# Attention over four batches: values times probabilities in four column tiles, row sums on GpSimd

## The chip, the cores and the metric

The kernel runs on one core of a Trainium2 chip, in f32 throughout. The metric is the time of one execution on the device in microseconds; the time before is the median of 3 runs, 4841.11 us (4838.23 to 4847.09).

The engines are called TensorE (PE in the profile, PEld for its weight loads), VectorE (DVE), ScalarE (ACT), GpSimd (POOL) and SyncE (SP, which here only issues DMAs). Each engine works its own queue in order.

## The reference

The reference is a chain of four residual layers on an input of 4 batches x 384 channels x 64 x 64. Only layer 0 and the part of layer 1 that runs beside it matter here. Layer 0, cut to what matters:

```python
xn  = layer norm over the 96 channels of x[:, :96]
qkv = einsum('oc,bchw->bohw', w_qkv, xn), scaled and shifted
q, k, v = 16, 16 and 96 channels, N = 4096 positions
attn = softmax(einsum('bcn,bcm->bnm', q, k) * scale, axis=-1)
out  = einsum('bcn,bmn->bcm', v, attn)
y    = w_proj @ relu(concat([out, x[:, 96:]])), scaled and shifted
x    = x + y
```

Layer 1 is a matrix product, a filter on 8 x 8 blocks in the Fourier domain, a depthwise 3 x 3 convolution with a gated GELU, and a second matrix product.

## The kernel before

`phase_a` runs layers 0 and 1. For each batch `b`, `side_by_side` interleaves two generators: `attention(b)`, which yields 64 times, and `others(b)`, which holds layer 1 of batch `b - 1` (`layer1`), the statistics of the next batch (`x_norm`) and its queries, keys and values (`qkv`). The order in which each engine gets its instructions is then set by a scheduler at build time, from dependences, priorities and its own estimates of cost. So batch 0 of attention runs beside little else, batches 1 to 3 run beside layer 1 of the batch before, and layer 1 of batch 3 runs alone at the end of the phase.

A step of `attention` is a pair (i, c): a block i of 512 query positions and a group c of 4 x 128 key positions. `scores` (L805) makes 4 matmuls of 32 rows each that run at once (L811), into one PSUM tile of four banks, and ScalarE takes the exponential of the halves into `probs`, a tile of 2048 columns in two buffers (L819). Scores are one step ahead of the products. The maximum is not subtracted inside the loop, so the softmax needs only a sum of the exponentials over the keys and one division per block.

Products and sums exist in two forms:

- Batches 1 to 3: four matmuls a step of 128 x 128 x 512 (L929). The stationary operand `vt` has 128 columns: 96 of values and 32 of ones (`wv` has ones in its last row and columns), so rows 96 to 127 of the result `av` hold the sum of the probabilities. At the end of a block `finish` (L897) takes the reciprocal of those rows (L901) and multiplies three quarters of `av` by it (L904). `av` alternates between the two PSUM buffers of tag "a".
- Batch 0: `products` (L827) computes the 96 value columns alone, as three pieces of 32 columns for each of the four groups of 128 keys, 12 matmuls a step. The four column tiles of TensorE work on four of them at once, in three rounds that `PLAN` sets out, into two PSUM tiles `av_0` and `av_1` (L834). The sum over the keys is made apart: `add_up` (L842) adds the two halves of `probs` into `acc_p` on VectorE (L848, L850, L851), and at the end of a block the two halves of that (L854). `evacuate` (L856) copies the pieces out of PSUM on ScalarE and VectorE (L860 to L863), `invert` (L866) sums `acc_p` over the partitions with ones (L870) and takes the reciprocal (L878), and `finish_tiles` (L881) spreads it by matmuls (L886), adds the pieces (L893) and multiplies (L894).

Both end in `layer0_end` (L949): ReLU of the other channels on ScalarE, three groups of three matmuls (L965), the addition to the residual on VectorE (L972), and a DMA issued by GpSimd (L975). These matmuls, those of layer 1 and those of `qkv` share one PSUM tag "m" with two buffers.

In `layer1`, `tile_norm` (L1043, VectorE), `tile_hidden` (L1051), `tile_filter` (L1066, L1068) and `tile_back` (L1076) fill a ring of three `bands`. `halo` copies rows between bands on GpSimd (L1089, L1090). `band_taps` applies nine taps for each of three channel blocks: the first on ScalarE (L1126), the others on VectorE (L1128: an instruction with two tensor inputs, band and acc). `band_out` multiplies, adds (L1148, L1149, L1152) and stores with a DMA issued by GpSimd (L1155).

At the end of the kernel, `boxes` adds rows with GpSimd (L2021, L2023) and VectorE (L2024 to L2034) side by side, and `conv7` builds band matrices on both (L1959).

Of the kernel before, what the change touches and what calls it, by code (L numbers as in the profile page):

```python
# [21 lines left out]
F32 = mybir.dt.float32  # L22
AF = mybir.ActivationFunctionType
ALU = mybir.AluOpType
# [4 lines left out]
NJ = 3  # L29
P = 128  # L30
PD = 96
# [250 lines left out]
class _Builder:  # L282
# [161 lines left out]
    def qkv_weights(self, pool):  # L444

        nc = self.nc
        w = self.wk("wq_raw", "lx", 2)[:, 0:PD]
        nc.scalar.dma_start(w, self.ins["w_qkv"])  # L450
        inv, shift = self.bn_scale_shift(
            "bn1", self.vec("bn1_m"), self.vec("bn1_v"), self.vec("bn1_g"), self.vec("bn1_b")
        )
        nc.vector.tensor_scalar(w, w, inv, None, ALU.mult)
        pt = self.pm("wq_pt")
        nc.tensor.transpose(pt[0:PD, 0:P], w, self.ident)
        wt = self.wk("wq_t", "ln", 3)[0 : PD + 1, 0:P]
        raw = self.wk("wq_rawt", "lx", 2)[0:PD, 0:P]
        nc.vector.tensor_copy(raw, pt[0:PD, 0:P])
        nc.vector.tensor_scalar(wt[0:PD, :], raw, self.vec("ln_w", PD), None, ALU.mult)  # L460
        pb = self.pm("wq_pb")
        nc.tensor.matmul(pb[0:1, 0:P], lhsT=self.vec("ln_b", PD), rhs=raw, start=True, stop=False)
        nc.tensor.matmul(pb[0:1, 0:P], lhsT=shift, rhs=self.ident, start=False, stop=True)
        nc.scalar.copy(wt[PD : PD + 1, :], pb[0:1, 0:P])

        self.wq4 = pool.tile([PD + 1, 4, 32], F32, tag="wq4", name="wq4")
        self.wk4 = pool.tile([PD + 1, 4, 32], F32, tag="wk4", name="wk4")
        self.wv = pool.tile([PD + 1, P], F32, tag="wv", name="wv")
        for t in (self.wq4, self.wk4, self.wv):
            nc.gpsimd.memset(t, 0.0)  # L470
        nc.gpsimd.memset(self.wk4[PD : PD + 1, :, 0:1], 1.0)
        nc.gpsimd.memset(self.wv[PD : PD + 1, PD:], 1.0)
        self.ones = pool.tile([P, 32], F32, tag="ones", name="ones")
        nc.gpsimd.memset(self.ones, 1.0)
        for g in range(4):
            nc.vector.tensor_copy(self.wq4[:, g, 1:17], wt[:, 0:16])
            nc.vector.tensor_copy(self.wk4[:, g, 1:17], wt[:, 16:32])
        nc.vector.tensor_copy(self.wv[:, 0:PD], wt[:, 32:P])
        self.wqk = pool.tile([PD + 1, 4, 32], F32, tag="wqk", name="wqk")
        nc.vector.tensor_copy(self.wqk[:, 0:3], self.wq4[:, 0:3])  # L480
        nc.vector.tensor_copy(self.wqk[:, 3], self.wk4[:, 3])
        self.score_bound(pool, wt)
# [220 lines left out]
    def qkv_tiles(self):  # L703


        q = [None] * 8
        k4 = self.big.tile([P, 8, P], F32, tag="k4", name="k4", bufs=2)
        vt = self.big.tile([P, 32, P], F32, tag="vt", name="vt", bufs=2)
        return q, k4, vt

    def qkv(self, b, q, k4, vt, tiles=(None,) * 8):
        nc = self.nc

        xc, xn = [None] * 8, [None] * 8
        xc[0] = self.centered(b, 0, tiles[0])
        yield 1.0
        xn[0] = self.layer_norm(xc[0])
        xc[1] = self.centered(b, 1, tiles[1])
        yield 2.0
        for i in range(8):  # L720
            if i + 2 < 8:
                xc[i + 2] = self.centered(b, i + 2, tiles[i + 2])
                yield 1.0
            if i + 1 < 8:
                xn[i + 1] = self.layer_norm(xc[i + 1])
                yield 1.0
            xa = xn[i]
            q[i] = self.big.tile([P, 512], F32, tag="q", name="q", bufs=9)
            m = self.pm("qk_m")
            nc.tensor.matmul(m, lhsT=self.wqk.rearrange("p g d -> p (g d)"), rhs=xa, start=True, stop=True)  # L730
            nc.scalar.copy(q[i][0:96], m[0:96])
            nc.scalar.copy(q[i][96:128], m[64:96])
            nc.sync.dma_start(
                q[i].rearrange("(g d) n -> g d n", g=4)[:, 0], self.shifts[b][:, i * 512 : (i + 1) * 512]
            )
            for g in range(4):
                nc.vector.tensor_copy(k4[32 * g : 32 * g + 32, i], m[96:128, g * P : (g + 1) * P])
            m = self.pm("v_m")
            mv = m.rearrange("p (c d) -> p c d", d=P)
            for c in range(4):  # L740
                nc.tensor.matmul(mv[:, c, :], lhsT=xa[:, c * P : (c + 1) * P], rhs=self.wv, start=True, stop=True)
            nc.vector.tensor_copy(vt[:, 4 * i : 4 * i + 4, :], mv)
            yield 2.8
# [14 lines left out]
    def maxima(self, b):  # L758
        nc = self.nc
        for _ in self.x_norm(b):  # L760
            pass
        q = self.big.tile([P, 32, P], F32, tag="vt", name="mx_q", bufs=2).rearrange("p (i a) n -> p i (a n)", i=8)
        q = [q[:, i] for i in range(8)]
        k = [self.probs.tile([P, 2048], F32, tag="p", name="mx_k") for _ in range(2)]
        for i in range(8):
            xa = self.layer_norm(self.centered(b, i))
            m = self.pm("mx_q_m")
            nc.tensor.matmul(m, lhsT=self.wq4.rearrange("p g d -> p (g d)"), rhs=xa, start=True, stop=True)
            nc.scalar.copy(q[i], m)
            m = self.pm("mx_k_m")  # L770
            nc.tensor.matmul(m, lhsT=self.wk4.rearrange("p g d -> p (g d)"), rhs=xa, start=True, stop=True)
            nc.vector.tensor_copy(k[i // 4][:, i % 4 * 512 : (i % 4 + 1) * 512], m)
        for i in range(8):
            mx = self.sm([P, 4, 2], "mx")
            for t in range(4):
                for u in range(2):
                    s = self.p4("mx_s")
                    for v in range(4):
# [4 lines left out]
                            start=True,  # L783
# [15 lines left out]
    def attention(self, b, q, k4, vt):  # L799
# [42 lines left out]
        def add_up(c, p):  # L842

            lo, hi = p[:, 0:1024], p[:, 1024:2048]
            if c == 0:
                t = self.blk.tile([P, NJ, 512], F32, tag="x", name="acc_p", bufs=1)
                self.acc = t[:, 0:2].rearrange("p a n -> p (a n)")
                nc.vector.tensor_add(self.acc, lo, hi)  # L848
            else:
                nc.vector.tensor_add(self.acc, self.acc, lo)  # L850
                nc.vector.tensor_add(self.acc, self.acc, hi)  # L851
            if c == 7:
                self.prob_sum = self.wk("sum_p", "acc", 5)
                nc.vector.tensor_add(self.prob_sum, self.acc[:, 0:512], self.acc[:, 512:1024])  # L854

        def evacuate(av):  # L856

            a, t = self.wk("av_a", "acc", 5), self.wk("av_t", "acc", 5)
            with tc.high_priority():
                nc.scalar.copy(t[0:32], av[0][96:128])  # L860
                nc.vector.tensor_copy(a[0:PD], av[0][0:PD])
                nc.scalar.copy(t[32:64], av[1][0:32])
                nc.vector.tensor_copy(t[64:96], av[1][32:64])  # L863
            return a, t
# [13 lines left out]
            nc.vector.reciprocal(rd, m[:, 0:P])  # L878
            return rd

        def finish_tiles(a, t, rd):  # L881

            xm = self.work.tile([P, NJ, 512], F32, tag="xm", name="xm", bufs=1)
            m = self.pm("rd_m")
# [9 lines left out]
            nc.vector.scalar_tensor_tensor(xm[0:PD, 0], t[0:PD], 0.0, m[0:PD], ALU.max, ALU.mult)  # L894
            return xm

        def finish(av):  # L897

            xm = self.work.tile([P, NJ, 512], F32, tag="xm", name="xm", bufs=1)
            rd = self.wk("av_rd", "rd", 1)  # L900
            nc.vector.reciprocal(rd[PD:P], av[PD:P])  # L901
            for g in range(3):
                at = slice(32 * g, 32 * g + 32)
                nc.vector.scalar_tensor_tensor(xm[at, 0], av[at], 0.0, rd[PD:P], ALU.max, ALU.mult)  # L904
            return xm

        st = self.stats_tile("xa_st")
        steps = [(i, c) for i in range(8) for c in range(8)]
        ahead = scores(*steps[0])
        done, end = None, iter(())  # L910
        close = finish if b else finish_tiles
        for n_step, (i, c) in enumerate(steps):
            p = ahead
            if n_step + 1 < len(steps):
                ahead = scores(*steps[n_step + 1])
            if b == 0:
                if c == 0:
                    av = self.pa("av_0"), self.pa("av_1")
                products(av, c, p)
                add_up(c, p)  # L920
                if c == 0 and done is not None:
                    done = *done, invert(self.prob_sum)
                if c == 7:
                    evacuated = evacuate(av)
            else:
                if c == 0:
                    av = (self.pa("av"),)
                for v in range(4):
                    nc.tensor.matmul(  # L929
                        av[0],  # L930
                        lhsT=vt[:, 4 * c + v, :],
                        rhs=p[:, v * 512 : (v + 1) * 512],
                        start=c == 0 and v == 0,
                        stop=c == 7 and v == 3,
                    )
                evacuated = av
            next(end, None)
            if c == 1 and done is not None:
                end = self.layer0_end(b, i - 1, close(*done), st)
            if c == 7:  # L940
                done = evacuated
            yield
        if b == 0:
            done = *done, invert(self.prob_sum)
        for _ in self.layer0_end(b, 7, close(*done), st):
            pass
        self.norm1 = self.norm_of_stats(st)

# [1153 lines left out]
```

## Time and profile before

| What | Value |
|---|---|
| Median of 3 runs | 4841.11 us |
| The profiled execution, its time | 4841.52 us |
| The profiled execution, its span | 4839.6 us |
| Attention, batch 0 | 40 to 458 us |
| Attention, batches 1, 2, 3 | 458 to 1017, to 1577, to 2139 us |
| Layer 1 of batch 3 alone | about 2139 to 2430 us |
| Granted TensorE clock, mean over the span | 0.95 |

In a table of stretches each row gives the start and end in us, the length, and for each engine its busy time with the number of instructions, then the granted TensorE clock, the busy share of the DMA engines and GB/s. In a group line stand the line of the kernel, the engine, the operation, the tile written and the tiles read, the shapes and the count, then the busy time in us, the mean ns of one, the idle time of the engine just before them, and what ended it. A line of a single source line gives the durations in ns as minimum/median/maximum and the first and last start. Every f32 matmul stands twice in the counts of TensorE.

### The profile page before, as it was taken

The page shows a single profiled execution, that of the slowest core. Times are in us where ns is not written, and L with a number is a line of the kernel's source. Part 1 is how long each engine was busy: PE and PEld are TensorE (multiplying, and loading weights), DVE is VectorE, ACT ScalarE, POOL GpSimd, SP SyncE. Part 2 cuts the span into 40 slices and gives each one's busy share as a digit, 9 for nine tenths or more (in the row PEclk, how much of TensorE's full clock was granted, in tenths as well). Part 3 has the DMA queues.
Part 4 walks back from the last instruction along what each step waited for, and adds up shares of the span by engine and source line. Part 5 has one row for each costly group of instructions (what it writes and reads, how often), then busy time and mean ns, then how long its engine had stood idle before and what let it go on. Part 6 is the DMA issues. An engine that isn't in the chain of part 4 may idle for free.

```text
span 4839.6 us, 49747 instructions
## 1 busy us (share of the span) xinstructions
PE 4399.5 (91%) x18445; PEld 2453.7 (51%) x18445; DVE 2892.0 (60%) x4647; ACT 1996.9 (41%) x2976; POOL 757.7 (16%) x643
## 2 busy tenths in 40 slices
PE   6999999999999999989987898699999997778888
PEld 2233444344443444435477787344444443678888
DVE  7766556645656455556867777555521113767898
ACT  4444444444444444336345566211133334763321
POOL 1000000000000000000044554000000001235544
PEclk9999999999999999989988999899999998788999
DMA  4312212111211111113168898776664444995776
GB/s 145 102 42 66 72 53 75 64 56 42 70 61 63 40 59 59 53 63 120 65 197 282 278 308 299 273 259 251 238 236 153 156 156 152 325 346 183 231 256 232
DMA packets 289663, 747.65 MB, mean 154 GB/s; under 512 B 22555, under 2 KB 123014, under 8 KB 277382
## 3 DMA queue, kind: packets, MB, share of 16 engines
q1 hardware_dynamic: 226744, 454.62, 29.4%
q0 software_dynamic: 36480, 167.01, 9.2%
q10 hardware_dynamic: 26190, 122.76, 6.4%
q8 instruction: 149, 2.44, 0.2%
q14 instruction: 100, 0.82, 0.1%
HBM read 442.04 MB, written 302.25 MB: 154 GB/s over the span
## 4 chain that ended last, share of the span: by engine, by line
PE 32%; DVE 7%; DMA 6%; ACT 3%; issue 2%; POOL 1%; SPq 0%; ACTq 0%; DVEq 0%; POOLq 0%
PE h_m L1658 10%; PE h_s L1604 10%; PE conv_m L1370 6%; PE conv_m L1972 2%; DMA c_d<-d 2%; DMA wmix<-in_mix_t 1%; DMA g_h<-h 1%; DVE toep L1959 1%; PE box_m L2050 1%; DVE in_x L2052 1%; DMA ax<-x 1%; DVE in_x L2062 1%; DMA unit_x<-x 1%; DVE box L2034 0%; ACT g_h L1908 0%
## 5 line engine op out<-in xcount | busy, mean ns | idle before, releaser
L819 ACT ACTIVATE probs<-sc_s 128x1024 f32<-128x1024 f32 x512 | 496.5, 1019 | 695.0 <-PE av L929 594.8
L929 PE MATMUL av<-probs,vt 128*128 128x512 f32 x1536 | 717.7, 604 | 0.0
L1128 DVE SCALAR_TENSOR_TENSOR acc<-band,vecs,acc 128x512 f32<-128x512 f32 x708 | 496.0, 745 | 44.9 <-POOL band L1089 39.6
L1658 PE MATMUL h_m<-f_h,cm_w_t 128*128 128x512 f32 x1152 | 497.3, 595 | 7.4 <-ACT f_h L1646 7.4
L1370 PE MATMUL conv_m<-toep,z 128*128 128x192 f32 (+1 forms) x2304 | 444.2, 354 | 9.5 <-DVE z L1299 9.4
L929 PEld LDWEIGHTS av<-probs,vt 128*128 128x128 f32 x1536 | 277.6, 192 | 339.6 <-issue 335.9
L1972 PE MATMUL conv_m<-toep,z 128*128 128x128 f32 x3072 | 395.5, 287 | 36.5 <-POOL toep L1959 15.8
L1370 PEld LDWEIGHTS conv_m<-toep,z 128*128 128x128 f32 x2304 | 408.5, 197 | 31.6 <-DVE z L1299 10.1
L1972 PEld LDWEIGHTS conv_m<-toep,z 128*128 128x128 f32 x3072 | 381.1, 203 | 38.4 <-POOL toep L1959 16.2
L1604 PE MATMUL h_s<-e_tok,cm_w_t 128*128 128x512 f32 x768 | 362.9, 595 | 4.2 <-DVE e_tok L1589 4.2
L1658 PEld LDWEIGHTS h_m<-f_h,cm_w_t 128*128 128x128 f32 x1152 | 220.4, 191 | 284.4 <-issue 273.3
L1666 DVE BATCH_NORM_STATS2 h_st<-f_h 128x6 f32<-128x512 f32 x96 | 66.5, 694 | 429.8 <-ACT f_h L1665 429.8
L811 PE MATMUL sc_s<-q,k 32*128 32x512 f32 x2048 | 307.1, 643 | 15.1 <-ACT probs L819 14.9
L1351 POOL TENSOR_TENSOR toep<-w,band 128x1280 f32<-128x1280 f32 x94 | 272.6, 2900 | 237.5 <-PE conv_m L1370 234.3
L1051 PE MATMUL t_m<-w_in_t,xb 128*128 128x384 f32 x768 | 282.0, 503 | 3.4 <-DVE coef L1068 3.2
L965 PE MATMUL proj_m<-xm,w_proj_t 128*128 128x512 f32 x576 | 270.3, 609 | 6.4 <-DVE xm L904 4.9
L1611 ACT COPY e_h<-h_s 128x1024 f32<-128x1024 f32 x96 | 97.2, 1012 | 400.2 <-PE h_s L1604 400.2
L1613 DVE BATCH_NORM_STATS2 h_st<-e_h 128x6 f32<-128x512 f32 x192 | 123.4, 685 | 204.9 <-ACT e_h L1611 204.7
L1604 PEld LDWEIGHTS h_s<-e_tok,cm_w_t 128*128 128x128 f32 x768 | 146.9, 191 | 187.9 <-issue 183.1
L1051 PEld LDWEIGHTS t_m<-w_in_t,xb 128*128 128x128 f32 x768 | 144.4, 194 | 141.6 <-issue 62.5
L972 DVE SCALAR_TENSOR_TENSOR x_res<-proj_m,bn_c,x_res 128x512 f32<-128x512 f32 x96 | 71.7, 747 | 240.2 <-PE proj_m L965 240.2
L1604 PE MATMUL h_s<-z,cm_w_t 128*128 128x512 f32 x384 | 196.7, 594 | 0.0
(423 smaller groups left out, 6396.3 us busy)
## 6 DMA issues: line engine op xcount, KB each, us to landing
d<-d_o ACTq DMA_DIRECT2D x48, 1024.0 KB
c_d<-d SPq DMA_DIRECT2D x48, 1024.0 KB
hid<-e_h ACTq DMA_DIRECT2D x16, 3072.0 KB
f_h<-hid SPq DMA_DIRECT2D x16, 3072.0 KB
x_in<-in_x SPq DMA_DIRECT2D x96, 256.0 KB
x_res<-in_x SPq DMA_DIRECT2D x32, 768.0 KB
xa<-x_res POOLq DMA_DIRECT2D x32, 768.0 KB, 3.9
xa_out<-xa SPq DMA_DIRECT2D x32, 768.0 KB
```

What stands on the lines that cost most here:

```text
L811: nc.tensor.matmul(s[:, g], lhsT=k4[32 * g : 32 * g + 32, c], rhs=q[i][32 * g : 32 * g + 32], start=True, stop=True,)
L819: nc.scalar.activation(p[:, h * 1024 : (h + 1) * 1024], s[:, 2 * h : 2 * h + 2].rearrange("p a b -> p (a b)"), AF.Exp, scale=0.25,)
L929: nc.tensor.matmul(av[0], lhsT=vt[:, 4 * c + v, :], rhs=p[:, v * 512 : (v + 1) * 512], start=c == 0 and v == 0, stop=c == 7 and v == 3,)
L965: nc.tensor.matmul(m, lhsT=self.w_proj[:, j, o * P : (o + 1) * P], rhs=xm[:, j], start=j == 0, stop=j == NJ - 1,)
L1051: nc.tensor.matmul(m[:, 0:C], lhsT=xb[:, j], rhs=self.w_in[:, j, :], start=j == 0, stop=j == NJ - 1,)
L1128: nc.vector.scalar_tensor_tensor(out, src(j, k), w, done, ALU.mult, ALU.add)
L1351: eng.tensor_tensor(t, self.w53[:, at : at + 160].rearrange("p (m n) -> p m n", n=8).unsqueeze(2).to_broadcast([P, 20, 8, 8]), band.rearra ...
L1370: nc.tensor.matmul(m[:, c * 256 + to : c * 256 + to + 64 * (k1 - k0)], lhsT=self.z_[:, at : at + P], rhs=t[:, 10 * c + k0 : 10 * c + k1].r ...
L1604: nc.tensor.matmul(s[:, v, :], lhsT=w1[:, j, o * P : (o + 1) * P], rhs=t[j][:, v * 512 : (v + 1) * 512], start=j == 0, stop=j == NJ - 1,)
L1613: nc.vector.bn_stats(st[:, o, 8 * b + 2 * i + v, :], h[:, o, v * 512 : (v + 1) * 512])
L1658: nc.tensor.matmul(m, lhsT=w2[:, o, j * P : (j + 1) * P], rhs=h[:, o, v * 512 : (v + 1) * 512], start=o == 0, stop=o == 5,)
L1972: nc.tensor.matmul(m[:, ch * P : (ch + 1) * P], lhsT=self.z_[:, at : at + P], rhs=t[:, 8 * c + 2 * i : 8 * c + 2 * i + 2].rearrange("p m a ...
```

## The change

All four batches take the form with column tiles. `wv` and `vt` lose the columns of ones and are 96 wide. `add_up` runs on GpSimd, apart from the lower half of each step but the first in batch 0, which stays on VectorE. Its accumulator and sum move to tiles of their own in the pool of `probs`. `finish` for batches 1 to 3 goes, `finish_tiles` takes its name, and in batches 1 to 3 the sum is inverted one step later than in batch 0 (`late`). `evacuate` uses tiles of other tags in the work pool. `maxima`, a branch that this input does not take, gets its tiles in another shape.

```diff
-        self.wv = pool.tile([PD + 1, P], F32, tag="wv", name="wv")
+        self.wv = pool.tile([PD + 1, PD], F32, tag="wv", name="wv")
...
-        nc.gpsimd.memset(self.wv[PD : PD + 1, PD:], 1.0)
...
-        vt = self.big.tile([P, 32, P], F32, tag="vt", name="vt", bufs=2)
+        vt = self.big.tile([P, 32, PD], F32, tag="vt", name="vt", bufs=2)
...
-            mv = m.rearrange("p (c d) -> p c d", d=P)
+            mv = m[:, 0 : 4 * PD].rearrange("p (c d) -> p c d", d=PD)
...
             if c == 0:
-                t = self.blk.tile([P, NJ, 512], F32, tag="x", name="acc_p", bufs=1)
-                self.acc = t[:, 0:2].rearrange("p a n -> p (a n)")
-                nc.vector.tensor_add(self.acc, lo, hi)
+                self.acc = self.probs.tile([P, 1024], F32, tag="acc", name="acc_p", bufs=1)
+                nc.gpsimd.tensor_add(self.acc, lo, hi)
             else:
-                nc.vector.tensor_add(self.acc, self.acc, lo)
-                nc.vector.tensor_add(self.acc, self.acc, hi)
+                for x in (lo, hi):
+                    (nc.vector if b == 0 and x is lo else nc.gpsimd).tensor_add(self.acc, self.acc, x)
             if c == 7:
-                self.prob_sum = self.wk("sum_p", "acc", 5)
-                nc.vector.tensor_add(self.prob_sum, self.acc[:, 0:512], self.acc[:, 512:1024])
+                self.prob_sum = self.probs.tile([P, 512], F32, tag="sum", name="sum_p", bufs=1)
+                nc.gpsimd.tensor_add(self.prob_sum, self.acc[:, 0:512], self.acc[:, 512:1024])
...
-            a, t = self.wk("av_a", "acc", 5), self.wk("av_t", "acc", 5)
+            a, t = self.wk("av_a", "rd", 1), self.wk("av_t", "av_t", 1)
...
-        def finish_tiles(a, t, rd):
+        def finish(a, t, rd):
...
-        def finish(av):
-
-            xm = self.work.tile([P, NJ, 512], F32, tag="xm", name="xm", bufs=1)
-            rd = self.wk("av_rd", "rd", 1)
-            nc.vector.reciprocal(rd[PD:P], av[PD:P])
-            for g in range(3):
-                at = slice(32 * g, 32 * g + 32)
-                nc.vector.scalar_tensor_tensor(xm[at, 0], av[at], 0.0, rd[PD:P], ALU.max, ALU.mult)
-            return xm
-
...
-        close = finish if b else finish_tiles
+        late = 1 if b else 0
...
-            if b == 0:
-                if c == 0:
-                    av = self.pa("av_0"), self.pa("av_1")
-                products(av, c, p)
-                add_up(c, p)
-                if c == 0 and done is not None:
-                    done = *done, invert(self.prob_sum)
-                if c == 7:
-                    evacuated = evacuate(av)
-            else:
-                if c == 0:
-                    av = (self.pa("av"),)
-                for v in range(4):
-                    nc.tensor.matmul(
-                        av[0],
-                        lhsT=vt[:, 4 * c + v, :],
-                        rhs=p[:, v * 512 : (v + 1) * 512],
-                        start=c == 0 and v == 0,
-                        stop=c == 7 and v == 3,
-                    )
-                evacuated = av
+            if c == 0:
+                av = self.pa("av_0"), self.pa("av_1")
+            products(av, c, p)
+            add_up(c, p)
+            if c == late and done is not None:
+                done = *done, invert(total)
+            if c == 7:
+                evacuated, total = evacuate(av), self.prob_sum
             next(end, None)
-            if c == 1 and done is not None:
-                end = self.layer0_end(b, i - 1, close(*done), st)
+            if c == late + 1 and done is not None:
+                end = self.layer0_end(b, i - 1, finish(*done), st)
```

More of the change, by code (lines that the diff above doesn't have):

```diff
@@ L477, in qkv_weights @@
             nc.vector.tensor_copy(self.wk4[:, g, 1:17], wt[:, 16:32])
-        nc.vector.tensor_copy(self.wv[:, 0:PD], wt[:, 32:P])
+        nc.vector.tensor_copy(self.wv, wt[:, 32:P])
         self.wqk = pool.tile([PD + 1, 4, 32], F32, tag="wqk", name="wqk")
@@ L761, in maxima @@
             pass
-        q = self.big.tile([P, 32, P], F32, tag="vt", name="mx_q", bufs=2).rearrange("p (i a) n -> p i (a n)", i=8)
-        q = [q[:, i] for i in range(8)]
+        q = [self.big.tile([P, 32, PD], F32, tag="vt", name="mx_q", bufs=2) for _ in range(2)]
+        q = [t.rearrange("p a n -> p (a n)")[:, 512 * i : 512 * i + 512] for t in q for i in range(4)]
         k = [self.probs.tile([P, 2048], F32, tag="p", name="mx_k") for _ in range(2)]
@@ L942, in attention @@
             yield
-        if b == 0:
-            done = *done, invert(self.prob_sum)
-        for _ in self.layer0_end(b, 7, close(*done), st):
+        for _ in self.layer0_end(b, 7, finish(*done, invert(total)), st):
             pass
```

## The prediction

> **What bounds the kernel now.** I read the page first, then the busy time of each engine in the three stretches that the change rewrites (batches 1, 2 and 3 of attention, 458 to 2139 us), then the groups and waits in them, then single lines of the late part of the kernel, where GpSimd already adds.
>
> ```profile
> span 4839.6 us, 49747 instructions
> PE 4399.5 (91%) x18445; PEld 2453.7 (51%) x18445; DVE 2892.0 (60%) x4647; ACT 1996.9 (41%) x2976; POOL 757.7 (16%) x643
> ...
> core 0: us, PE busy (x) PEld busy (x) DVE busy (x) ACT busy (x) POOL busy (x), PEclk, DMA share, GB/s
> 458.00:1017.00 559.00, 541.21 (x1784) 235.08 (x1784) 333.69 (x579) 234.21 (x303) 24.19 (x46) 0.99 0.20 67
> 1017.00:1577.00 560.00, 544.07 (x1804) 237.35 (x1800) 325.18 (x566) 238.69 (x311) 20.20 (x39) 0.99 0.18 59
> 1577.00:2139.00 562.00, 546.87 (x1787) 237.40 (x1784) 299.71 (x493) 231.00 (x293) 19.51 (x37) 0.98 0.16 54
> ```
>
> TensorE is busy for 97% of each batch, VectorE for 53 to 60%, GpSimd for 4%. A batch has 64 steps, so a step takes 8.75 us. On average TensorE is the bound and GpSimd is free. The average hides this:
>
> ```profile
> 1440.00:1460.00 20.00, 20.00 (x70) 8.72 (x72) 5.84 (x5) 9.49 (x12) 0.72 (x1) 1.00 0.22 79
> 1470.00:1500.00 30.00, 25.02 (x74) 9.66 (x73) 25.74 (x40) 16.39 (x22) 1.33 (x3) 0.92 0.20 67
> ```
>
> When a band of the depthwise taps (L1128) comes up, VectorE is nearly full for about 20 us and TensorE, whose queue is in order, already idles. There are about eight such stretches in a batch.
>
> ```profile
> L1128 DVE SCALAR_TENSOR_TENSOR acc<-band,vecs,acc 128x512 f32<-128x512 f32 x572 | 394.9, 744 | 41.8 <-POOL band L1089 39.6
> L901 DVE RECIPROCAL av_rd<-av 32x512 f32<-32x512 f32 x23 | 77.4, 3364 | 60.8 <-PE av L929 60.6
> L834 PE MATMUL av<-probs,vt x1536: 592/593/1064, 63.7 to 456.1; 128*32 128x512 f32 x192
> L1959 POOL TENSOR_TENSOR toep<-wmix,band x63: 2332/2358/3084, 4080.7 to 4823.8; 128x1024 f32<-128x1024 f32 x63
> L2023 POOL TENSOR_TENSOR box<-box x48: 1258/1271/2249, 4354.4 to 4792.3; 128x512 f32<-128x512 f32 x48
> L2034 DVE SCALAR_TENSOR_TENSOR box<-in_x,off,box x48: 604/740/2840, 4371.3 to 4805.7; 128x512 f32<-128x512 f32 x36, 128x384 f32<-128x384 f32 x12
> L2024 DVE TENSOR_TENSOR box<-box,box x48: 660/690/2882, 4367.2 to 4803.2; 128x512 f32<-128x512 f32 x48
> ```
>
> The last three show a cost of GpSimd adds that the share of busy time doesn't: next to an add of 1.27 us, VectorE instructions of 0.7 us have taken up to 2.8 us, and an add up to 2.25. Of the L2034 instructions, those that overlap an add have a median of 1.9 us, the others 0.74.
>
> **What the skill says.** The Trainium skill, "SBUF — State Buffer", Who interferes with whom: a VectorE instruction with two SBUF inputs and a GpSimd instruction that reads SBUF exclude each other for the whole instruction. L2034 and L2024 agree. L1128 is such an instruction (band and acc both in SBUF), and so is every new add. "GPSIMD Engine Reference", 3.1: a two-input add costs about twice VectorE's; here 2.36 us (L1959, 1024 wide) against 1.22 (L850). "TensorEngine Tiling (Array Packing)", Key Properties: changing the tiling mode drains the array. The trace agrees: from the last matmul of one mode to the first of another the start distance is 0.52 us where the columns alone take 0.43, so 0.095 us a change.
>
> **The change, part by part, batches 1 to 3 (192 steps).**
>
> TensorE. Every f32 matmul appears as two passes; a pass of 512 columns starts 0.43 us after the one before. Removed: 4 matmuls a step at L929, 8 passes, 3.43 us. Added: 12 matmuls on 32-column tiles, four at once, 6 passes, 2.57 us. In batch 0, where this form runs already, a block goes from 217.91 to the next matmul at 220.62, 2.71 us with its mode changes. Gross: 192 x 0.86 = **-165 us**. The instruction order that the changed kernel is built with then takes most of it back:
> - It puts scores (or a few other matmuls) into the middle of a block of 12 and breaks a round of four: 26, 27 and 28 times in the three batches. A broken round costs one more, 81 x 0.86 = **+69 us**. A full-width product loses nothing by that.
> - Mode changes: 780 against 382, 398 x 0.095 = **+38 us**.
> - New per block of 512 columns: 4 matmuls of sum_m (at once, 2 passes of 0.107) and 4 of rd_m (8 passes), 1.07 us x 24 = **+26 us**. Values are 96 wide instead of 128: **-3 us**.
>
> Sum on TensorE: **-35 us**, 0.18 us a step instead of 0.86.
>
> VectorE. Removed per block: a reciprocal of 3.36 and three L904 of 0.68, 5.4 us. Added, with the durations of batch 0: two copies out of PSUM, an add and the final multiply at 0.69 each and a reciprocal of 0.95, 3.7 us. 24 x 1.7 = **-41 us**, off TensorE's path except in the full stretches.
>
> GpSimd. Added per batch: 120 adds of 1024 columns at 2.36 us and 8 of 512 at 1.27, 293 us, 4.6 us a step. With its halo copies, memsets and DMA issues (20 us) it is 56% busy, so it isn't the bound. Its adds are also not late for the probabilities: the exponentials of a step are done about a step and a half before its products, so two adds have some 10 us before they hold up the buffer that L819 waits for (now the wait is on the products, L929). Behind the adds in its in-order queue stand the halo copies (L1089), for which the taps wait: now 39.6 us in all. One add of delay in half of 24 bands is 28 us of VectorE; I take **+10 us** on TensorE, 0 to +40.
>
> The exclusion. I put an add at every moment of batches 1 to 3 of the trace and asked how long the next two-input VectorE instruction would be held: 35% of the adds hold one, the mean is 0.6 us. That is 0.6 x 120 = 72 us a batch, 216 us. It falls into the full stretches: inside one, roughly a third of the time is instructions without two SBUF inputs, 0.4 us before the next L1128, so an add holds VectorE for about 1.96 us. A stretch so lengthened meets more adds; I take 265 us. Less the 41 saved, VectorE's chain in the stretches grows by 224 us. How much reaches TensorE isn't shown anywhere in this trace. From below: TensorE's run-ahead and the idle VectorE between stretches hide most (0.15, 34 us); from above: all, since TensorE already idles in these stretches (224 us and the 41). I take half: **+112 us**. Less than nothing is excluded, since an add only takes time from VectorE.
>
> A new wait. The two accumulators av_0 and av_1 now take both buffers of their tag, so a block's first products wait for the copies of the last. Batch 0 shows 18 us of that (L863, L861) in 8 blocks, 2.25 us each; 24 x 2.25 = 54 if nothing is between, 0 if other matmuls cover it (about 1 us of them are queued there, but the copies stand behind taps on VectorE). I take **+25 us**.
>
> Batch 0. GpSimd takes 64 of the 120 adds and the 8 sums; VectorE loses 64 x 1.22 + 8 x 0.69 = 84 us of work. Waits of TensorE for L850 and L851 go (about 11 us), but each VectorE add now waits for GpSimd's of the step before, which ended long before. **-5 us**, -12 to +10. Issue of DMAs is the same in number and queue; SP's order doesn't move.
>
> Sum: -35 + 10 + 112 + 25 - 5 = **+107 us**. The profiled execution took 4841.5 us (span 4839.6), 0.4 us from the median of the runs: **4948 us**.
>
> **The rivals.**
> 1. *The exclusion hides; TensorE's gain comes through* (faster). Place: the stretches; VectorE idles 41% of a batch. Then -35 - 5, and with the long reciprocals gone perhaps 10 of the 17 us that TensorE idles per batch: 4790 to 4810, say 4801. It decides if less than some 20% of the hold time reaches TensorE and the accumulator copies are covered. Against it: 25.0 of 30 us at 1470.
> 2. *VectorE and GpSimd take turns all the time.* If the one-input L1043 (0.34 us x 96 a batch) also excludes adds, exclusive time per batch is 293 + 154 + 33 = 480 us of about 545, and queues grow on both; adds then become late, L819 waits for GpSimd and scores for L819. All of the hold time, 54 and 40 us: 5080 to 5120.
> 3. *About no change*: broken rounds overlap after all (-69) or half of the hold as assumed is a quarter. 4840 to 4880.
>
> **How the numbers follow.** My forecast, slower by 0.8 to 4.5%: 0.64. Rival 1: 0.12. Rival 2: 0.10. Rival 3: 0.14, of which 0.04 within 0.2% (10 us, about what a measurement of this kernel can tell from no change) and the rest slower. So faster 0.12, same 0.04, slower 0.84. The range leaves out rival 1 and half of rival 2's upper end: 4835 to 5085.
>
> **What would show it.** Right: products of batches 1 to 3 busy about 2.7 to 3.1 us a step instead of 3.74; L1128 (there L1101) with a mean well above 0.744 us and a maximum near 3; VectorE busy over 70% of a batch; TensorE's busy share down from 97% to about 90%, its waits ending on VectorE; GpSimd adds at 2.36 us or a little more. Wrong: L1101 still at 0.744, TensorE still at 97% and batches of about 548 us (rival 1); L819 waiting for GpSimd adds (rival 2).

## The result and the profile after

The changed kernel takes **5065.36 us** (median of 4 runs, 5050.52 to 5082.65), the kernel before 4844.1 us beside it: a ratio of 1.0464 [1.0444, 1.0484], slower by 221 us. The forecast was 107 us slower. The profiled execution is the slowest of the four, 5082.65 us with a span of 5080.9 us.

The page's head and the three stretches of batches 1 to 3 (479 to 2378 us), to be laid beside those of before:

```profile
span 5080.9 us, 57572 instructions
...
PE 4450.6 (88%) x21901; PEld 2362.6 (47%) x21901; DVE 3102.2 (61%) x4599; ACT 2023.8 (40%) x3024; POOL 1849.3 (36%) x1098
```

```profile
core 0: us, PE busy (x) PEld busy (x) DVE busy (x) ACT busy (x) POOL busy (x), PEclk, DMA share, GB/s
479.00:1137.00 658.00, 569.59 (x2963) 208.82 (x2962) 434.80 (x597) 250.05 (x330) 333.48 (x177) 0.94 0.18 59
1137.00:1785.00 648.00, 567.77 (x2988) 209.60 (x2987) 423.83 (x582) 252.51 (x335) 333.91 (x171) 0.94 0.15 51
1785.00:2378.00 593.00, 522.32 (x2848) 189.57 (x2851) 386.31 (x483) 223.30 (x286) 325.86 (x158) 0.94 0.14 48
```

The batches take 658, 648 and 593 us, each from its first product to that of the next, the last to its last product; before they took 574, 571 and 535. (By its products, the kernel before has its batches 1 to 3 from 459 to 1033, to 1604 and to 2139 us. The ends 1017 and 1577 in the table of before cut the same stretch nearly in thirds, and the shares read from them hold for these as well.) That is +219 us, against +221 between the medians. In the profiled execution itself batch 1 also starts 20 us later; TensorE's clock became full at 78 us there, at 34 us before. TensorE's busy share fell from 97% to 87 or 88%, and the granted clock from 0.98 or 0.99 to 0.94. GpSimd is busy for about half of a batch and VectorE for 65%.

The groups that the change and the prediction name, and the taps' source line (minimum, median, maximum in ns), with that of the normalisation before:

```profile
L849 POOL TENSOR_TENSOR acc_p<-acc_p,probs 128x1024 f32<-128x1024 f32 x392 | 970.1, 2475 | 869.0 <-ACT probs L818 657.8
L833 PE MATMUL av<-probs,vt 128*32 128x512 f32 x6144 | 812.4, 612 | 6.6 <-DVE av_t L861 6.6
...
L1101 DVE SCALAR_TENSOR_TENSOR acc<-band,vecs,acc 128x512 f32<-128x512 f32 x708 | 697.3, 1024 | 38.3 <-POOL band L1062 28.0
...
L1016 DVE TENSOR_SCALAR xb<-xa_in,gn_pg,gn_r 128x128 f32<-128x128 f32 x288 | 181.3, 679 | 115.5 <-PE t_m L1024 74.5
```

```profile
L1101 DVE SCALAR_TENSOR_TENSOR acc<-band,vecs,acc x708: 645/744/2911, 569.9 to 2655.5; 128x512 f32<-128x512 f32 x177
L1043 DVE TENSOR_SCALAR xb<-xa_in,gn_pg,gn_r x288: 329/341/396, 479.5 to 2004.8; 128x128 f32<-128x128 f32 x144
```

The products (L833) are busy for 812 us in 256 steps, 3.2 us a step; in batches 1 to 3 alone it is 3.26. A tap (L1101) has the old median, 0.744 us, but a mean of 1.024 and a maximum of 2.91. The one-input normalisation L1016 (L1043 before) has a mean of 0.679 against the 0.34 of an undisturbed one. ScalarE's exponentials (1.02 us) and a single matmul of the products (0.59 us) have the medians that they had before.

TensorE's waits in batches 1 to 3 now end mostly on VectorE: 186 of its 239 us of idle time, before 17 of 49. The largest entries now, and below them the largest of before, for ScalarE:

```profile
engine line waited for: us in total, times, longest us
PE coef_m L1039 <- DVE x_res L945: 42.6, 14, 5.4
PE coef_m L1039 <- DVE av_rd L876: 35.5, 6, 8.3
PE sc_s L810 <- ACT probs L818: 25.5, 15, 5.6
PE t_m L1024 <- DVE coef L1041: 19.8, 9, 5.2
...
PE rd_m L884 <- DVE coef L1041: 17.0, 3, 11.4
```

```profile
PE back_m L1076 <- ACT t_t L1059: 15.3, 9, 2.1
```

One such wait, on the timeline (start, length, engine, line; idle time in brackets), and TensorE and clock in the same stretch:

```profile
start us, us, engine line op out<-in xcount [idle before <-releaser]
...
1163.22 4.78 POOL L849 TENSOR_TENSOR acc_p<-acc_p,probs 128x1024 f32<-128x1024 f32 x2 [1.36 <-ACT probs L818]
1164.07 5.54 DVE L1016 TENSOR_SCALAR xb<-xa_in,gn_pg,gn_r 128x128 f32<-128x128 f32 x8
...
1171.07 0.16 DVE L435 TENSOR_TENSOR gn_d<-gn_d,gn_mv 128x3 f32<-128x3 f32 x1
...
1171.38 0.56 PE L419 MATMUL gn_pv<-gn_d,group 128*128 128x3 f32 x2 [5.01 <-DVE gn_d L435]
```

```profile
core 0: us, PE busy (x) PEld busy (x) DVE busy (x) ACT busy (x) POOL busy (x), PEclk, DMA share, GB/s
1164.00:1170.00 6.00, 2.19 (x12) 0.68 (x12) 5.94 (x10) 0.00 (x0) 3.92 (x2) 1.00 0.00 0
1170.00:1177.00 7.00, 5.62 (x15) 2.46 (x16) 2.88 (x16) 0.50 (x2) 0.00 (x0) 0.51 0.36 115
```

Two GpSimd adds run from 1163.22 us. Eight normalisations that take 2.7 us by themselves take 5.5 beside them. The small VectorE operations behind them in the queue come late, and TensorE waits 5.0 us, up to 1171.38 us, for the last of them, `gn_d`; 2.8 of the 5.0 us are what the eight took longer than by themselves. Its clock is lowered at 1170 us, late in the pause, and stays at one half for 6.8 us.

To find the 219 us I took three sums over batches 1 to 3 from the trace's records, for this kernel and those of the experiments: TensorE's busy time weighted with its granted clock (its **work**), its **idle** time, and what the clock takes (busy time less work). The **held** time of VectorE is what each instruction took above the median of the same instruction in the kernel without adds, counted where the excess is over 0.1 us.

| Kernel | Batches 1–3, us | Work | Idle | Clock | Held |
|---|---|---|---|---|---|
| before | 1680 | 1611 | 49 | 20 | – |
| after | 1899 | 1580 | 239 | 80 | 334 |
| e1 no adds in batches 1 to 3 | 1647 | 1578 | 61 | 8 | 22 |
| e2 full width, GpSimd adds | 1948 | 1644 | 222 | 82 | 312 |
| e3 memsets for adds | 1669 | 1578 | 76 | 15 | 118 |
| e4 adds on VectorE | 1675 | 1583 | 79 | 14 | 0 |
| e5 half the adds | 1771 | 1579 | 135 | 58 | 170 |
| e6 normalisation on ScalarE | 1871 | 1581 | 204 | 86 | 256 |
| e9 VectorE adds, chained | 1674 | 1553 | 99 | 22 | 0 |
| e10 as e9, normalisation on ScalarE | 1665 | 1548 | 91 | 25 | 0 |
| e11 GpSimd adds, chained | 1919 | 1552 | 277 | 90 | 322 |
| e12 narrow GpSimd adds | 1863 | 1578 | 208 | 77 | 278 |

From before to after: work -31, idle +190, clock +60, together +219.

### The profile page after: what moved, and what is told of

The parts are those of the page before. It is cut to its first block, busy times and chain, and to the rows that moved or that the text cites. A ratio compares the mean times of both kernels' runs of the same rounds, so it can differ in the third digit from the quotient of the medians.

```text
span 5080.9 us, 57572 instructions
## 1 busy us (share of the span) xinstructions
PE 4450.6 (88%) x21901; PEld 2362.6 (47%) x21901; DVE 3102.2 (61%) x4599; ACT 2023.8 (40%) x3024; POOL 1849.3 (36%) x1098
## 5 line engine op out<-in xcount | busy, mean ns | idle before, releaser
L849 POOL TENSOR_TENSOR acc_p<-acc_p,probs 128x1024 f32<-128x1024 f32 x392 | 970.1, 2475 | 869.0 <-ACT probs L818 657.8
L833 PE MATMUL av<-probs,vt 128*32 128x512 f32 x6144 | 812.4, 612 | 6.6 <-DVE av_t L861 6.6
L818 ACT ACTIVATE probs<-sc_s 128x1024 f32<-128x1024 f32 x512 | 496.5, 1020 | 581.2 <-PE av L833 470.4
L1101 DVE SCALAR_TENSOR_TENSOR acc<-band,vecs,acc 128x512 f32<-128x512 f32 x708 | 697.3, 1024 | 38.3 <-POOL band L1062 28.0
L833 PEld LDWEIGHTS av<-probs,vt 128*32 128x32 f32 x6144 | 185.4, 111 | 497.0 <-issue 458.7
L810 PE MATMUL sc_s<-q,k 32*128 32x512 f32 x2048 | 320.2, 664 | 30.2 <-ACT probs L818 30.2
L1024 PE MATMUL t_m<-w_in_t,xb 128*128 128x384 f32 x768 | 304.6, 533 | 24.4 <-DVE coef L1041 19.8
L1016 DVE TENSOR_SCALAR xb<-xa_in,gn_pg,gn_r 128x128 f32<-128x128 f32 x288 | 181.3, 679 | 115.5 <-PE t_m L1024 74.5
```

The costliest lines, as they stand in the source:

```text
L810: nc.tensor.matmul(s[:, g], lhsT=k4[32 * g : 32 * g + 32, c], rhs=q[i][32 * g : 32 * g + 32], start=True, stop=True,)
L818: nc.scalar.activation(p[:, h * 1024 : (h + 1) * 1024], s[:, 2 * h : 2 * h + 2].rearrange("p a b -> p (a b)"), AF.Exp, scale=0.25,)
L833: nc.tensor.matmul(av[k][quarter(g)], lhsT=vt[:, 4 * c + v, quarter(s)], rhs=p[:, v * 512 : (v + 1) * 512], start=c == 0 and not before, s ...
L849: (nc.vector if b == 0 and x is lo else nc.gpsimd).tensor_add(self.acc, self.acc, x)
L1024: nc.tensor.matmul(m[:, 0:C], lhsT=xb[:, j], rhs=self.w_in[:, j, :], start=j == 0, stop=j == NJ - 1,)
L1101: nc.vector.scalar_tensor_tensor(out, src(j, k), w, done, ALU.mult, ALU.add)
```

## The experiments

All are edits of the changed kernel; the code below is cut to the lines that matter. e1, e3 and e5 leave out part or all of the sums, so their output is not the reference's. The theory throughout: TensorE's work falls as forecast, and GpSimd's adds take VectorE's time in the full stretches, for which TensorE waits.

### The adds left out, and the columns left out

```diff
 # e1: GpSimd's adds of batches 1 to 3 left out after each block's first
-                for x in (lo, hi):
+                for x in (lo, hi) if b == 0 else ():
 # e2: products of batches 1 to 3 at full width, adds kept
+            if b:
+                for v in range(4):
+                    nc.tensor.matmul(av[0][0:PD], lhsT=vt[:, 4 * c + v, :],
+                                     rhs=p[:, v * 512 : (v + 1) * 512], ...)
+                return
...  (one accumulator, one copy of it by VectorE, no addition of pieces)
```

> The changed kernel; in batches 1 to 3 GpSimd adds only the first step of each block (1 add of 1024 columns per block instead of 15), so the sums of the probabilities leave out seven steps of eight. Everything on TensorE stays. Exclusion theory (the adds hold VectorE, TensorE idles and its clock falls): with the adds gone the taps are back at 0.744 us and TensorE keeps its own gain of about 32 us and loses only to the wait for the accumulators' copies: 4800 to 4835 us. Column-tile theory (broken rounds, mode changes, the wait for av_0 and av_1 are what costs): stays at 5000 us or more.

> The changed kernel with the column tiles undone in batches 1 to 3: four matmuls of 96 columns a step into one accumulator, as before, with the two PSUM buffers alternating; the adds on GpSimd and the division stay. Exclusion theory: TensorE has about 35 us more work than in the changed kernel and no wait for the accumulators, the adds hold VectorE as much: 5050 to 5110 us. Column-tile theory: close to the kernel before, 4840 to 4890 us.

Without the adds: 4811.67 us, 0.9937 [0.9909, 0.9966] of before. With the adds and full-width products: 5097.34 us, 1.0525 [1.05, 1.055]. So without the adds the change gains about 30 us (16 to 44 by the interval), close to the prediction's 35 on TensorE (in the table: work -33, idle +12, clock -12). With the adds in both, the column tiles gain about as much: e2 is 0.6% slower than the changed kernel. The adds cost all of the loss: 254 us between e1 and the changed kernel. The taps of e1 are nearly back at their old mean:

```profile
L1101 DVE SCALAR_TENSOR_TENSOR acc<-band,vecs,acc 128x512 f32<-128x512 f32 x708 | 515.1, 768 | 45.8 <-POOL band L1062 31.6
```

### What it is about the adds: GpSimd's time, or what it reads

```diff
 # e3: a ScalarE copy of one column, then memsets, for the two adds
+                if b:
+                    nc.scalar.copy(self.acc[:, 0:1], hi[:, 0:1])
+                    for _ in range(4):
+                        nc.gpsimd.memset(self.acc, 1.0)
...
 # e4: all adds of batches 1 to 3 on VectorE
-                    (nc.vector if b == 0 and x is lo else nc.gpsimd).tensor_add(self.acc, self.acc, x)
+                    (nc.vector if b or x is lo else nc.gpsimd).tensor_add(self.acc, self.acc, x)
...  (the same for a block's first add and for sum_p)
```

> The changed kernel; in batches 1 to 3 each step's two adds of GpSimd after the first are replaced by four memsets of the same 1024 columns (about 4 us together against 4.7), which start when the step's exponentials are there but read nothing from SBUF, and one ScalarE copy of one column; the sums are then constants. GpSimd stays about as busy. Exclusion theory: only instructions that read count, so within 25 us of the kernel without adds: 4800 to 4860 us. Occupancy theory (halo copies and DMA issues stand behind busy GpSimd): near the changed kernel, 5000 us or more.

> The changed kernel with all adds of batches 1 to 3 on VectorE instead of GpSimd. VectorE gets 120 x 1.22 + 8 x 0.69 = 152 us more a batch and is 85% busy, with nothing held. Exclusion theory: the same kind of lengthening, 152 us a batch where the adds on GpSimd held VectorE for 112, so as slow or slower unless the scheduler, which knows this work, places it between the stretches: 4900 to 5100 us, likeliest 4980. If GpSimd's own lateness is the cause, this is clearly faster than the changed kernel, below 4900.

Memsets: 4838.58 us, ratio 0.9995 [0.9981, 1.0009]. GpSimd is busy for about 270 us a batch (326 to 334 with the adds), and only 27 us of the 254 remain. So it isn't that GpSimd is occupied. Beside a memset the taps keep their median of 0.74 us; beside an add of the changed kernel it is 1.97. A memset (0.96 us) is shorter than an add (2.36), but that is not the reason, for adds of 1.27 us hold the taps too (e12, below). GpSimd's halo copies, which read SBUF like the adds, do hold a tap, if only briefly: one that starts 0.1 us into such a copy of 0.35 us takes 0.80 us. So of the GpSimd instructions here those that read SBUF hold the taps. The groups (mean after the bar) show a second thing:

```profile
L851 POOL MEMSET acc_p<- 128x1024 f32 x672 | 644.1, 958 | 683.4 <-ACT acc_p L849 655.1
L1105 DVE SCALAR_TENSOR_TENSOR acc<-band,vecs,acc 128x512 f32<-128x512 f32 x708 | 519.3, 774 | 41.6 <-POOL band L1066 29.6 <-ACT acc L1103 6.9
L1020 DVE TENSOR_SCALAR xb<-xa_in,gn_pg,gn_r 128x128 f32<-128x128 f32 x288 | 136.6, 638 | 120.3 <-PE t_m L1028 85.9 <-DMA xa_in<-xa 34.2
```

The taps are at 0.774 us, but the normalisation (here L1020) is at 0.638, and beside a memset its median is 0.92 us against 0.34 alone. It is held by memsets as well as by adds.

Adds on VectorE: 4855.77 us, 1.0028 [1.0014, 1.0041]. I had expected 4980; this was a miss, and the result under 4900 is the one that the expectation gave to lateness of GpSimd. e3 has answered that: GpSimd nearly as busy costs 27 us. VectorE is busy for 391 us more than in e1 (3184.6 against 2793.2 us on the pages), and the time rises by 44 us; in batches 1 to 3 of the traces it is 28 us, of which TensorE's idle time is 18:

```profile
core 0: us, PE busy (x) PEld busy (x) DVE busy (x) ACT busy (x) POOL busy (x), PEclk, DMA share, GB/s
478.00:1051.00 573.00, 543.60 (x2963) 199.96 (x2962) 460.82 (x724) 249.76 (x331) 29.93 (x48) 0.99 0.21 68
1051.00:1623.00 572.00, 547.62 (x2989) 203.00 (x2988) 451.30 (x711) 252.97 (x336) 23.71 (x43) 0.99 0.17 58
1623.00:2153.00 530.00, 504.79 (x2850) 184.67 (x2848) 406.68 (x601) 223.36 (x286) 16.65 (x31) 0.99 0.16 54
```

VectorE is 77 to 80% busy there and TensorE 95 to 96%. So VectorE had room for the work. It isn't that these adds stay out of the stretches where VectorE is full: 102 of 335 adds start while taps run (pauses between taps of up to 1.5 us counted in), and in the changed kernel 100 of 336. In slices of 10 us VectorE is at least 90% busy in 60 of 167, and in 62 of 189 of the changed kernel. But in such a slice TensorE idles 0.8 us with the adds on VectorE and 3.0 us with them on GpSimd. So a full VectorE does not by itself stop TensorE. A likely reason is that the build-time scheduler counts adds on VectorE when it orders the queues, and does not count a hold; no run here shows it, and the cause of this difference stays open.

### The dose

```diff
 # e5: only the lower half of each step added on GpSimd
-                for x in (lo, hi):
+                for x in (lo, hi) if b == 0 else (lo,):
 # e12: each add as two of 512 columns
...
+                    for h in (slice(0, 512), slice(512, 1024)):
+                        nc.gpsimd.tensor_add(self.acc[:, h], self.acc[:, h], x[:, h])
```

> The changed kernel with half the GpSimd adds in batches 1 to 3: of each step after the first only the lower half is added (65 instead of 120 adds of 1024 columns a batch; the output leaves out part of each row's sum). Theory A (every add holds VectorE for about the same time and VectorE has no spare time in the full stretches): the loss against the kernel without adds is proportional, 0.54 of 254 us, so 4812 + 137 = 4949 us, and VectorE's held time falls from 336 to about 180 us. Rival B (a threshold: the idle time of VectorE swallows the first part, and only what is over it reaches TensorE): 4860 to 4895 us at about the same 180 us of held time. Rival C (the first adds already cost most, because any add that strikes a full stretch idles TensorE and lowers its clock): above 5000 us.

> The changed kernel with each GpSimd add of batches 1 to 3 after a block's first split into two of 512 columns (1.27 us each instead of 2.36), the same bytes read. Theory (an add shuts a two-input VectorE instruction out until the add ends): the longest L1101 falls from 2.9 us to about 2.0, VectorE gets in between the halves, its held time falls from 336 to some 240 us and the time to about 5000 us. Rival (what counts is the bytes that GpSimd reads while VectorE wants them): the held time stays within 10% of 336 us and the time at 5050 to 5090 us.

Half the adds: 4932.33 us, 1.0186 [1.016, 1.0211]. Held time is 170 us, 51% of the full kernel's, and the loss over e1 is 121 us, 48%. At this dose there is no threshold: the loss is in proportion.

```profile
L1101 DVE SCALAR_TENSOR_TENSOR acc<-band,vecs,acc 128x512 f32<-128x512 f32 x708 | 598.4, 885 | 42.1 <-POOL band L1062 33.3
```

Narrow adds: 5028.79 us, 1.0396 [1.0368, 1.0424], between the two theories. Held time falls by a sixth, to 278 us, in more and shorter pieces (190 taps at 0.9 us over their usual, where there were 110 at 1.8):

```profile
L853 POOL TENSOR_TENSOR acc_p<-acc_p,probs 128x512 f32<-128x512 f32 x672 | 917.6, 1396 | 594.1 <-ACT probs L818 591.7 <-ACT gn_r L374 2.0
L1105 DVE SCALAR_TENSOR_TENSOR acc<-band,vecs,acc 128x512 f32<-128x512 f32 x708 | 666.3, 981 | 39.0 <-POOL band L1066 31.6 <-ACT acc L1103 2.2
```

An add of 512 columns lets VectorE in sooner, but the next one of a step is there at once. The maximum of a tap stayed at 2.84 us, against my 2.0: the taps of over 2 us all stand beside a block's first add, which is still 1024 wide.

### The one-input instruction

```diff
 # e6: normalisation of a tile on ScalarE in all batches
-            if alone:
+            if True:
```

> The changed kernel with all adds kept, and the normalisation of a tile in layer 1 (L1016, one input in SBUF, 96 a batch) on ScalarE in all batches as it already is in the part of layer 1 that runs alone. It takes 98 us of plain duration and 98 us of held time off VectorE in batches 1 to 3. Theory A (the one-input instruction is held by the adds like the others and its hold reaches TensorE in the same share): 5065 - 0.6 x 98 for the hold and some of the 98 us of plain work with it, 4950 to 5005 us, and the held time of L1101 stays near 200 us. Rival B (its long durations only reflect that it sits in the full stretches; the two-input taps take over what it leaves): 5040 to 5070 us, with the held time of L1101 up by nearly 98. A loss (over 5080) would say that ScalarE, now behind with exponentials, is the bound.

5040.19 us, 1.041 [1.0386, 1.0434]: some 26 us less than the changed kernel (by the ratios), at the border of the second theory, whose other mark, more held time on the taps, came only to 11 us (mean 1.041 after 1.024). Held time fell by 78 us and VectorE's own work by 98, and little of it reached TensorE. The same move without GpSimd adds gained 11 us (e10 against e9, below; 16 by the ratios). So the hold on the normalisation is real, but little of it is on TensorE's path; in e6 the other holds, 234 us over e1's, go with 221 us of idle and clock.

### A version that keeps the gain

```diff
 # e9: as e4, and scores and products chained (e10: as e9, and e6's edit; e11: the chain, adds on GpSimd)
...
+            behind = tc.issue_after(self.last_product.ins) if b and self.last_product else nullcontext()
+            with behind, tc.high_priority() if b else nullcontext():
...
-            products(av, c, p)
+            with tc.issue_after(self.last_score.ins) if b else nullcontext():
+                products(av, c, p)
 # e7: as e4, and each block's products in a critical section (e8: as e7, and e6's edit)
-            products(av, c, p)
+            with tc.tile_critical() if b else nullcontext():
+                products(av, c, p)
```

> All adds of batches 1 to 3 on VectorE, and the 12 matmuls of a block kept together, so that no round of four is broken by other matmuls (0 instead of about 75). Theory: TensorE then has 75 x 0.86 = 64 us less to do than with the adds on VectorE alone (4856 us), and mode changes fall too; if TensorE is the bound, 4785 to 4800 us, faster than the kernel before (4843). Rival: VectorE, at over 70% of a batch with the adds, holds the pace: 4835 to 4860 us. If keeping the block together makes TensorE wait for the whole block's inputs and adds instructions to its queue: over 4870 us.

> As e7_vector_whole, and the normalisation of a tile in layer 1 on ScalarE in all batches, which takes 98 us off VectorE in batches 1 to 3. If VectorE's work is what keeps e7 from its TensorE sum: 15 to 40 us below e7. If TensorE is the bound in e7: within 8 us of it. If ScalarE's exponentials come late by it: above e7.

5412.98 us (1.1172 [1.115, 1.1194]) and 5377.29 us (1.1095 [1.1072, 1.1117]): the worst of all, as the third branch for e7 said. e8 is 36 us under e7, within the 15 to 40 foretold for VectorE's work being in the way. Part of the loss stands in TensorE's waits: products are put down as waiting for DMAs of layer 1 that they don't use. That the section gathers foreign waits at its head is inferred from this:

```profile
engine line waited for: us in total, times, longest us
PE av L833 <- issue: 105.7, 42, 7.7
...
PE av L833 <- DMA xa_out<-xa: 33.2, 7, 6.3
PE av L833 <- DMA x_res<-in_x: 32.2, 6, 6.4
```

> All adds of batches 1 to 3 on VectorE, and the scores chained behind the last product issued and the products behind the last score, so that scores no longer fall into a block of products: 48 instead of 85 broken rounds and 662 instead of 775 mode changes in the three batches. By the prices of the prediction TensorE has 37 x 0.86 + 113 x 0.095 = 43 us less to do. Theory (TensorE is the bound here, a broken round costs a whole one): 4856 - 43 = 4813 us, faster than the kernel before (4843). Rival (the gain goes into waits, since scores come later and ScalarE's exponentials with them): 4835 to 4870 us.

> As e9_vector_chained, with the normalisation of a tile in layer 1 on ScalarE in all batches (98 us less on VectorE in batches 1 to 3, about 110 more on ScalarE). Beside e9 it shows what that move costs or brings where no GpSimd add is there. Theory A (e6 gained only 25 us because the instruction was not on TensorE's path, held or not): within 10 us of e9. Rival B (e6 gained some 75 us on VectorE and lost 50 by later exponentials on ScalarE): 25 to 50 us above e9.

> The changed kernel, adds on GpSimd, with the same chaining: 52 instead of 81 broken rounds, 684 instead of 773 mode changes, 29 x 0.86 + 89 x 0.095 = 33 us less for TensorE. If TensorE's own work still adds to the time though it idles 80 us a batch: about 5032 us. If the held VectorE alone sets the pace: 5055 to 5070 us.

e9: 4844.23 us, 1.0023 [1.0011, 1.0035]. e10: 4833.06 us, 0.999 [0.9979, 1.0002]. e11: 5088.24 us, 1.0526 [1.0508, 1.0544]. The chain takes 30 us (e9 against e4) and 27 us (e11 against after) off TensorE's work, where the prices 0.86 and 0.095 gave 43 and 33. TensorE's idle time takes 20 and 37 us back, the clock 9 and 10. For e9 the rival held; e10 came out 11 us below e9, just outside its theory A (within 10 us) and far from its rival; e11 was outside both theories. That with VectorE held a fixed order leaves TensorE fewer other matmuls to turn to would explain e11, but is not shown. e10 is the best version that keeps all of the sums; it can't be told from the kernel before.

## Why the prediction was right in direction and wrong in size

The total lay inside the range of 4835 to 5085 us, but above the 0.8 to 4.5% that was called likeliest: +107 us were forecast, +221 (4.6%) measured. By its steps:

- **TensorE, -35.** Measured -31 us of work (1611 to 1580). Right as a sum. Its parts were tested in two places: against full-width products (e2) the column tiles take off 64 us of work, where gross gain, broken rounds and mode changes gave 58; and the chained kernels save 70 to 80% of what the prices of broken rounds and mode changes gave together.
- **Batch 0, -5.** Not seen. The thirteen kernels with the changed batch 0 take 415 to 430 us from the first scores to the first product of batch 1; before it was 418. A gain of 5 us can't be told in that.
- **GpSimd and the halo, +10; accumulators, +25.** Too large. The taps' wait for the halo fell from 39.6 to 28.0 us, and memsets that keep GpSimd busy nearly as long cost 27 us, with the hold on the normalisation in it. Without adds, with the accumulators as they are, TensorE idles only 12 us longer than before.
- **The exclusion, +112.** The step that failed is this term of the sum: it measured 251 us in place of 112 (changed kernel against e1), 179 of idle time and 72 of clock. Its first factor, 265 us of hold on two-input instructions, came near: 236 us without the normalisation. (One reading behind it was off: the VectorE instructions of over 2 us that it puts beside adds of 1.27 us all stand beside adds of 2.36 us, L1959.) It left out the normalisation, 98 us in 60 of 288, which stood only as an "if" in the second rival; the page of the Trainium skill that the prediction named, "SBUF — State Buffer", Who interferes with whom, has the case in the same list: a VectorE instruction in a mode that uses both ports excludes a GpSimd instruction, without regard to what that reads, and `tensor_scalar` is among those that can run so. e3 agrees, with 0.92 us beside a memset against 0.34. The second factor, "I take half" after 41 us of saved VectorE work, was a guess. Against e1, 312 us of hold go with 179 us more idle time, 0.57, so the half came near by luck; but it was taken of 224 us and not of 312, and no gain from the saved work shows (e1, with the wait for the accumulators in it, idles 61 us, before 49). That makes 67 of the missing 139 us. The other 72 are the clock.
- **The clock.** The prediction has no term for it, and from before to after it is 60 us (e1 to after 72). The Trainium skill, "TensorE: Matmul & The Clock Gate", What's actually happening, says that the clock halves after an idle window of about 3.4 us. Here each lowered stretch lasts 3.4 us or a multiple of it, at 0.50, but shorter pauses than the page's bring it on: each of the 36 stretches in batches 1 to 3 began in or after a pause that filled at least 2.2 of the 3.5 us before, and in the kernel before 1.8 was enough. Pauses of over 2 us went from 14 to 42, in e1 to 5; the lowered stretches from 11 to 36, in e1 to 3. Such a pause was followed by a lowered stretch in 36 of 42 cases, before in 8 of 14. So a pause of this size often costs its own length and then half of the speed for 3.4 us or more. The five rows of the table with over 200 us of idle time have 77 to 90 us of clock, the seven others 8 to 58; but no run changed the clock alone, so that it follows the pauses is read from the traces.

Together: idle +190 where the waits were put at 147 (10 + 112 + 25), clock +60 where nothing was put, work as forecast.

**The rivals.** The first fell with the exclusion; e1 at 4812 shows what it would have been. (Its 4801 is -35 and -5 alone; of the 10 us per batch that it names, 30 in all, there is nothing in it.) The second (5080 to 5120) lay above the measured 5065, and its own terms, 224 us of hold, 54 and 40 less 35 and 5, come to its upper end. It had the right extra instruction, but not the path: L818 waited for an add 4 times, 14.2 us in all, and taking the normalisation off VectorE gave back only 26 us. The third fell. Of the marks foretold two failed: VectorE over 70% of a batch (it was 65%: its hold adds to its busy time, but the batch grew with it), and products of 2.7 to 3.1 us a step (3.26; in e1, with nearly the full clock, 3.14).

## What to carry to other kernels

Price an idle engine's work by what its instructions shut out on its neighbour: here GpSimd's adds held VectorE for 334 us in three batches and that cost TensorE some 250 us, while the same adds put openly on VectorE, 391 us of busy time, cost 44. Why shut-out time cost so much more than open work is not settled. Count for the hold all of the neighbour's instructions that lengthen beside it, not only those with two tensor inputs (here the one-input normalisation had 98 of the 334 us, though little of that reached TensorE), and reckon with a lowered clock at pauses of TensorE of over about 2 us. A sum that a wide matmul carries along for nothing (the columns of ones) is hard to beat: all that the column tiles freed was 30 us, and no way tried here of making the sum again left a measurable part of it.

## What the runs showed that I had not expected

- A memset on GpSimd holds VectorE's one-input normalisation of a tile in SBUF (median 0.34 to 0.92 us), but not its two-input taps (0.74 and 0.74).
- VectorE is the loser of most meetings: the 392 adds of L849 have a mean of 2.475 us over a median of 2.358, some 46 us of delay, nearly all in batches 1 to 3, beside 334 us on VectorE there.
- VectorE can be as full without TensorE waiting for it: 0.8 us of idle time in a full slice of 10 us in e4, 3.0 in the changed kernel.
